# A fused attention and expert kernel: attention's features transposed on VectorE from raw rows, row deviation applied after the products, K's elu as a sum on GpSimd

## The chip, the cores and the metric

The kernel runs on one core of a Trainium2 chip, in one launch. Its time is the device time of that core, in microseconds (us), from the first to the last instruction and what lies around them; the median of several runs counts. The engines are PE (TensorE, matrix products and transposes), DVE (VectorE), ACT (ScalarE), POOL (GpSimd) and SP (SyncE, which here only issues DMAs). Each works through its own instructions in program order.

## The reference

For 16 batches of 1024 tokens with 256 features, a row is normalized, and a linear attention with 16 heads of 16 and a layer of 8 experts are both added to the raw row:

```
xn  = (x - mean(x)) / sqrt(var(x) + 1e-5)
Q, K = elu(xn Wq' + bq) + 1, elu(xn Wk' + bk) + 1 ;  V = xn Wv' + bv
attn = per head  Q (K' V) / (Q . sum(K) + 1e-6),  then Wo' + bo
probs = softmax(xn gate_w)                  # over the 8 experts
g, m  = top 256 tokens of each expert in each batch, by probs
ffn[m] += g * (gelu(xn[m] w1[e]) w2[e])     # scatter-add over experts
out = x + attn + ffn
```

All inputs and the output are 32-bit floats.

## The kernel before

**Attention** runs first, one batch per step, `step(b)` for b from -1 to 16. It is a software pipeline: in step b the K products and the gate are made for batch b+1 (`next_`), Q, the denominators and K'V for batch b (`here`), the output for b-1 (`prev`), and the row statistics, the normalized rows and their transposes for b+2 (`ahead`). x of b+3 is loaded. Products with V's and the output's weights are folded into 256x256 matrices (`folded_k`, `folded_v`, `folded_o`).

The order on every engine is written out by hand: within `tc.manual_schedule` each engine keeps the order of the calls. The names that matter: `moments` (L272) and `deviations` (L276 to L281: aggregation and the negated mean on DVE, the deviation by a power on POOL), `normalize` (L295, ACT), `transpose_x` (L306 on PE, L311 copies out of PSUM on ACT) makes `xnT`, in which the features lie on the partitions; `key` (L319 PE, L323 DVE: bias added while reading PSUM) fills `kk`, whose last 8 columns are the gate's logits; `exp_of` (L328, L329) makes exp(min(t, 0)) in two ACT operations; `elu` (L333, DVE) takes the larger of that and t+1, the 1 being part of the bias; `gate_exp` and `gate` (L341 to L357) do the softmax on DVE with its exponent on ACT, and SP stores the row with its probabilities; `key_sum` (L366 to L368, POOL) adds K over the tokens; `query` (L388 PE, L393 DVE), `query_keys` (L401, POOL), `divide` (L409 to L413 on DVE, L415 on POOL), `folded_k` (L424), `transpose_q` (L470, L473), `project` (L494, L500). The DVE part of a step is in this order: K's reads with the moments between them, deviations, gate's maximum, elu of K's first half, gate, Q's first read, elu of K's second half, Q's second read, third read, elu of Q's first half, fourth read, elu of Q's second half, the two divisions, the outputs.

From step 3 to step 14, rounds of the top-k search of the first four batches (L188 to L193, on DVE) are put in between, eight instructions a step (`top`). PSUM has eight banks, which are handed out in rotation by `bank`.

**Experts.** 64 units follow, each one expert with 2 batches. A unit gathers 512 rows by indirect DMA on POOL (`gather`, L238), SP regroups them in blocks of 32 partitions (`quadrants`, L712), DVE transposes 32x32 blocks (`transposed`, L721), and both layers are done by a seven-product scheme (`layer1` L798, `layer2` L877), whose sums lie on DVE and POOL (`fourth_sum`, L863, feeds the last product of `layer2`). The result, weighed on ACT (L894), is added into `acc` in DRAM by indirect DMA on POOL (`scatter`, L900). `plan` places the pieces of the output (x + attention + bias + acc, in parts of 256 rows: `load_a`, `cast` L1017, `bias` L1021, `add` L1026, `store` L1030) into slots of the units ("s1" to "s4", "first", "middle", "lay"). The parts of the last unit's batches wait for its scatters and a reload of `acc` (`load_last_a`, L1013).

Of the kernel before, what the change touches and what calls it, by code (L numbers as in the profile page):

```python
# [23 lines left out]
def tile_linear_attn_expert_choice_moe(  # L24
# [72 lines left out]
    wo_sb = const.tile([P, NC, E], F32, name="wo_sb")  # L97
    bqc = const.tile([P, NC], F32, name="bqc")
# [4 lines left out]

    def load_first_weights():
        nc.scalar.dma_start(wkg_sb[:, :, 0:E], wkT.rearrange("(c p) o -> p c o", p=P))
        nc.scalar.dma_start(wkg_sb[:, :, E:KG], gate_w.rearrange("(c p) e -> p c e", p=P))
        nc.gpsimd.memset(bk_sb[:, E:KG], 0.0)
        nc.scalar.dma_start(bk_sb[:, 0:E], bk.partition_broadcast(P))

    def load_other_weights():  # L110
        nc.sync.dma_start(wq_sb, wqT.rearrange("(c p) o -> p c o", p=P))
# [4 lines left out]
        nc.sync.dma_start(bo_sb, bo.partition_broadcast(P))  # L116


    def add_one():
        nc.gpsimd.tensor_scalar(bk_sb[:, 0:E], bk_sb[:, 0:E], 1.0, None, ALU.add)  # L120

    def spread_bq(diag):

        for c in range(NC):
            nc.vector.tensor_scalar(diag[:, c, :], ident, bqc[:, c : c + 1], None, ALU.mult)
# [6 lines left out]
    def load_w1(g, e):  # L132
        w1_sb = wpool.tile([P, NC, HID], F32, tag="w1", name=f"w1_{g}_{e}")

        wq4 = w1[e].rearrange("(q c i) f -> q i c f", q=4, c=NC)
        for q in range(4):
            nc.sync.dma_start(w1_sb[32 * q : 32 * q + 32, :, :], wq4[q])
# [107 lines left out]
    def attention(xpool, apool, tpool, zpool, first_units):  # L245
# [3 lines left out]
        class Batch:  # L249
            def __init__(self, b):  # L250
                self.b = b

        def load_x(t):
# [4 lines left out]
            for g in range(2):  # L258
                nc.sync.dma_start(
                    t.x[g],  # L260
                    x[t.b].rearrange("(j p) d -> p j d", p=P)[:, 4 * g : 4 * g + 4, :],
                )

        def new_stats(t):
# [3 lines left out]
            t.rstd = tpool.tile([P, NJ], F32, tag="rstd", name=f"rstd{t.b}")  # L268
# [31 lines left out]
        def transpose_x(t, g):  # L300
            if g == 0:
                t.xnT = xpool.tile([P, NC, S], F32, tag="xnT", name=f"xnT{t.b}")
            for c in range(NC):
                pt = bank(f"xt{t.b}_{g}_{c}")
                for j in range(4):
                    nc.tensor.transpose(  # L306
# [4 lines left out]
                nc.scalar.copy(t.xnT[:, c, g * 512 : (g + 1) * 512], pt)  # L311


        def key(t, j):
# [3 lines left out]
            for d in range(NC):  # L318
                nc.tensor.matmul(  # L319
                    pk[:, 0:KG], t.xnT[:, d, j * P : (j + 1) * P], wkg_sb[:, d, :],  # L320
                    start=(d == 0), stop=(d == NC - 1),
                )
            nc.vector.tensor_tensor(t.kk[:, j, :], pk[:, 0:KG], bk_sb, ALU.add)  # L323


        def exp_of(t, name, g, of):
            e = tpool.tile([P, 4, E], F32, tag="e", name=f"{name}e{t.b}_{g}", bufs=3)
            nc.scalar.activation(e, of, AF.Relu, bias=1.0, scale=-1.0)  # L328
# [3 lines left out]
        def elu(of, e):  # L332
            nc.vector.tensor_tensor(of, of, e, ALU.max)  # L333

# [892 lines left out]
```

## Time and profile before

| | |
|---|---|
| median of 3 runs | 2173.39 us (2169.7 to 2173.79) |
| profiled execution | 2174.56 us, its span 2172.8 us |
| TensorE clock granted | 0.994 of full speed |
| attention | 0 to about 556 us; steps 3 to 13 take 33.53 us each |
| experts | from 558 us |
| last product of layer 2 ends | about 2146.3 us |

A line of a timeline gives the start and duration in us, the engine, the line of the kernel, the operation, what is written and read, and the shapes; in brackets stands how long the engine had been idle and what released it. In the windows, the first two numbers are the stretch and its length, then the busy time of PE, PE's weight loads, DVE, ACT and POOL with the number of instructions, the granted clock, the share of DMA time and GB/s.

### The profile page before, as it was taken

What the parts mean: (1) busy time and instruction counts of PE and PEld (TensorE: products, weight loads), DVE (VectorE), ACT (ScalarE), POOL (GpSimd) and SP (SyncE); (2) the same over time, 40 slices, a digit from 0 to 9 for tenths busy, and PEclk for the clock granted to TensorE, in tenths of its full rate; (3) what the DMA queues carried; (4) which work ended last, traced back from release to release, by engine and by line L of the source; (5) the groups of instructions that cost most, each with busy time, mean ns of one, the idle gap of its engine ahead of it and who ended that gap; (6) DMA issues with size and microseconds to landing.
All of it is one profiled execution on the core that took longest, in us unless ns stands there. A gap on an engine that the chain in (4) does not pass through costs nothing.

```text
span 2172.8 us, 37223 instructions
## 1 busy us (share of the span) xinstructions
PE 2125.9 (98%) x13556; PEld 1958.3 (90%) x13556; DVE 1754.6 (81%) x3197; ACT 860.9 (40%) x1599; POOL 1354.7 (62%) x1015
## 2 busy tenths in 40 slices
PE   7999999999999999999999999999999999999995
PEld 6888888888899998999999999899999999999994
DVE  6888888887799888679999998767777788777786
ACT  5645546453333333333333333333333333333334
POOL 4545445454677777677666766676676667667743
PEclk9999999999999999999999999999999999999998
DMA  6444535455555555454565556445546665565567
GB/s 200 138 146 147 188 125 176 156 161 173 122 108 103 104 113 124 102 122 94 135 137 118 119 133 135 77 92 106 115 103 165 166 156 115 132 140 106 117 168 213
DMA packets 333767, 290.61 MB, mean 134 GB/s; under 512 B 163856, under 2 KB 285968, under 8 KB 333584
## 3 DMA queue, kind: packets, MB, share of 16 engines
q1 hardware_dynamic: 283168, 217.55, 35.3%
q0 software_dynamic: 49728, 70.29, 18.5%
q8 instruction: 107, 1.75, 0.4%
q14 instruction: 76, 0.62, 0.1%
q10 hardware_dynamic: 688, 0.40, 0.1%
HBM read 153.36 MB, written 101.19 MB: 117 GB/s over the span
## 4 chain that ended last, share of the span: by engine, by line
PE 97%; DVE 1%; DMA 1%; issue 0%; ACT 0%; POOL 0%; SPq 0%; POOLq 0%; DVEq 0%; ACTq 0%
PE pb L798 15%; PE qz L877 11%; PE qx L877 11%; PE pc L798 10%; PE pa L798 10%; PE pk L319 5%; PE qv L877 5%; PE qw L877 5%; PE qy L877 5%; PE pq L388 5%; PE pg L424 5%; PE po L494 5%; PE xt L306 1%; PE qt L470 1%; PE pv L439 1%; PE pm L458 1%
## 5 line engine op out<-in xcount | busy, mean ns | idle before, releaser
L900 POOL DMA_INDIRECT acc<-y,idxT x256 | 414.9, 1621 | 349.8 <-ACT y L894 172.5
L238 POOL DMA_INDIRECT rows<-xg,idxT x256 | 261.4, 1021 | 77.6 <-issue 69.4
L894 ACT ACTIVATE y<-y,rows 128x256 f32<-128x256 f32 (+1 forms) x256 | 102.5, 448 | 516.1 <-DVE y L932 514.7
L773 ACT ACTIVATE hT<-hT 128x512 f32<-128x512 f32 x384 | 237.9, 630 | 154.5 <-DVE hT L830 92.0
L798 PE MATMUL pb<-ts,ws 128*128 128x256 f32 x1024 | 264.7, 381 | 1.9 <-DVE ts L748 1.2
L798 PE MATMUL pa<-xT,w 128*128 128x256 f32 x1024 | 263.7, 380 | 1.1 <-issue 1.1
L877 PE MATMUL qx<-w,hT 128*128 128x128 f32 x2048 | 249.5, 275 | 0.0
L877 PEld LDWEIGHTS qx<-w,hT 128*128 128x128 f32 x2048 | 243.9, 192 | 3.3
L863 POOL TENSOR_TENSOR sums<-hT,sums 128x512 f32<-128x512 f32 x128 | 172.3, 1363 | 96.6 <-PE qz L877 96.2
L798 PEld LDWEIGHTS pb<-ts,ws 128*128 128x128 f32 x1024 | 195.3, 191 | 29.3 <-POOL wt L767 1.6
L798 PEld LDWEIGHTS pa<-xT,w 128*128 128x128 f32 x1024 | 190.2, 191 | 24.6 <-issue 1.3
L828 DVE TENSOR_TENSOR u<-pb,p 128x512 f32<-128x512 f32 x128 | 88.4, 691 | 114.9 <-PE pb L798 99.6
L773 ACT ACTIVATE hT<-pa 128x512 f32<-128x512 f32 x128 | 76.4, 597 | 177.2 <-PE pa L798 175.8
L819 DVE TENSOR_TENSOR u<-pb,p 128x512 f32<-128x512 f32 x128 | 88.5, 691 | 65.6 <-ACT y L894 41.4
L812 ACT COPY p<-pa 128x512 f32<-128x512 f32 x128 | 74.9, 585 | 166.3 <-PE pa L798 157.5
L798 PE MATMUL pc<-xT,ws 128*128 128x256 f32 x512 | 134.7, 385 | 0.9 <-DVE hT L830 0.9
L798 PE MATMUL pc<-ts,ws 128*128 128x256 f32 x512 | 132.7, 382 | 0.0
L798 PE MATMUL pb<-ts,w 128*128 128x256 f32 x512 | 131.4, 379 | 0.0
L877 PE MATMUL qz<-w,sums 128*128 128x128 f32 x1024 | 124.9, 275 | 0.0
L877 PE MATMUL qw<-wt,hT 128*128 128x128 f32 x1024 | 124.8, 275 | 0.0
L877 PE MATMUL qz<-wt,sums 128*128 128x128 f32 x1024 | 124.8, 275 | 0.0
L877 PE MATMUL qv<-wt,hT 128*128 128x128 f32 x1024 | 124.8, 275 | 0.0
(145 smaller groups left out, 4747.6 us busy)
## 6 DMA issues: line engine op xcount, KB each, us to landing
rq<-rows SPq DMA_DIRECT2D x1024, 32.0 KB
w<-in_w_dram SPq DMA_DIRECT2D x96, 256.0 KB
w<-in_w_dram SPq DMA_DIRECT2D x48, 512.0 KB
xg<-xn SPq DMA_DIRECT2D x16, 1056.0 KB
x<-in_x_dram SPq DMA_DIRECT2D x32, 512.0 KB
acc<-zero SPq DMA_DIRECT2D x16, 1024.0 KB
xr<-in_x_dram SPq DMA_DIRECT2D x30, 512.0 KB
xa<-xr SPq DMA_DIRECT2D x28, 512.0 KB
```

The source lines that it names most:

```text
L238: nc.gpsimd.indirect_dma_start(out=rows[:, q, :], out_offset=None, in_=xg[b], in_offset=bass.IndirectOffsetOnAxis(ap=ix, axis=0),)
L319: nc.tensor.matmul(pk[:, 0:KG], t.xnT[:, d, j * P : (j + 1) * P], wkg_sb[:, d, :], start=(d == 0), stop=(d == NC - 1),)
L388: nc.tensor.matmul(pq[:, k * E : (k + 1) * E], t.xnT[:, d, j * P : (j + 1) * P], wq_sb[:, d, :], start=(d == 0), stop=(d == NC - 1),)
L424: nc.tensor.matmul(t.pg[:, c * E : (c + 1) * E], t.xn[:, j, c * P : (c + 1) * P], t.kk[:, j, 0:E], start=(j == 0), stop=(j == NJ - 1),)
L494: nc.tensor.matmul(po[:, k * E : (k + 1) * E], qT[:, c, j * P : (j + 1) * P], t.mo[:, c, :], start=(c == 0), stop=(c == NC - 1),)
L773: nc.scalar.activation(out, in_, AF.Gelu_apprx_tanh)
L798: nc.tensor.matmul(bk[:, j * HT : (j + 1) * HT], w[:, f * P : (f + 1) * P], x, start=start and j == 0, stop=True, skip_group_check=True,)
L819: nc.vector.tensor_tensor(u2, both(pb), p1, ALU.add)
L863: nc.gpsimd.tensor_tensor(u.half_sum(0, r), u.block(1, 0, r), u.half_sum(1, r), ALU.subtract)
L877: nc.tensor.matmul(bk[:, k * EH : (k + 1) * EH], a[:, c, k * P : (k + 1) * P], b[:, c, :], start=start and k == 0 and c == 0, stop=True, s ...
L894: nc.scalar.activation(y[:, k, cols], in_, AF.Copy, scale=rows[:, q, E + u.e : E + u.e + 1])
L900: nc.gpsimd.indirect_dma_start(out=acc[b], out_offset=bass.IndirectOffsetOnAxis(ap=ix, axis=0), in_=y[:, k, :], in_offset=None, compute_op ...
```

## The change

In attention, for batches from 2 on, `xnT` is no longer made from normalized rows on PE. x is loaded a second time by `load_blocks`, in runs of 64 features (256 bytes) to blocks of 32 partitions, and `transpose_blocks` lets DVE transpose 32x32 blocks of it; so `xnT` holds raw x. The mean is taken out of the weights instead: `center` subtracts the mean over the input features from each column of second copies of Wk, gate and Wq. The deviation `rstd` of a row is multiplied in by `of_tokens` when K and Q are read from PSUM. Batches 0 and 1 keep the old way with the uncentered copies. K's elu becomes relu(t) + exp(min(t, 0)): `split_key` does three ACT operations, and `elu_key` the sum, on POOL (on DVE in step -1).

At the start, x of batch 0 is loaded in quarters, its statistics are taken in pairs of row groups, `warm_up` puts matmuls of ones on PE ahead of the first transposes, and the second half's transposes follow the first half's K. At the turn to the experts, the second gather moves behind the divisions, the third in front of the second layer's weight sums, and the first expert's w1 is loaded a step later. At the end, the last unit doesn't scatter: `new_hot` and `fill_hot` make one-hot matrices of its token indices in earlier units (`iota` on POOL, a comparison on DVE), `spread` multiplies them with the unit's result on PE, and DVE adds `acc`, which is loaded before that. The last unit's `fourth_sum` runs on DVE, and some biases, additions and stores move into it.

The diff, cut to its core:

```diff
+    def load_in_blocks(queue, tile_, w):
+        w4 = w.rearrange("(q c i) f -> q i c f", q=4, c=NC)
+        for q in range(4):
+            queue.dma_start(tile_[32 * q : 32 * q + 32, :, :], w4[q])
+
+
+    def center(w, n):
+        pb = bank("pw")
+        for c in range(NC):
+            nc.tensor.matmul(
+                pb[:, 0:n], ones, w[:, c, :], start=(c == 0), stop=(c == NC - 1)
+            )
+        for c in range(NC):
+            nc.vector.scalar_tensor_tensor(
+                w[:, c, :], pb[:, 0:n], -1.0 / E, w[:, c, :], ALU.mult, ALU.add
+            )
...
+        load_in_blocks(nc.sync, wkg_sb[:, :, 0:E], wkT)
+        load_in_blocks(nc.sync, wkg_sb[:, :, E:KG], gate_w)
+        load_in_blocks(nc.sync, wq_sb, wqT)
...
+            n = 2 if t.b == 0 else 4
+            for j in range(0, NJ, n):
...
+                    t.x[j // 4][:, i : i + n, :],
+                    x[t.b].rearrange("(j p) d -> p j d", p=P)[:, j : j + n, :],
+                )
+
+        def load_blocks(t):
+
+
+            t.blocks = wpool.tile([P, NC, HID], F32, tag="w1", name=f"xb{t.b}").rearrange(
+                "p c (s d) -> p (c s) d", d=E // 4
+            )
+            x4 = x[t.b].rearrange("(s i) (q d) -> q i s d", i=32, q=4)
+            for q in range(4):
+                nc.sync.dma_start(t.blocks[32 * q : 32 * q + 32, :, :], x4[q])
+
+        def transpose_blocks(t, g):
+            if g == 0:
+                t.xnT = xpool.tile([P, NC, S], F32, tag="xnT", name=f"xnT{t.b}")
+            n = S // 64
+            for c in range(NC):
+                nc.vector.transpose(
+                    t.xnT[:, c, g * 512 : (g + 1) * 512].rearrange("p (s i) -> p s i", i=32),
+                    t.blocks[:, g * n : (g + 1) * n, 32 * c : 32 * c + 32],
                 )
...
+        def warm_up(n):
+            for _ in range(n):
+                nc.tensor.matmul(warm[:, 0:P], ones, ones, start=True, stop=True)
...
+                    if t.b == 0 and g == 0 and c == 0 and j > 1:
+                        warm_up(3)
...
+                t.pt[c] = pt
+                if copies:
+                    copy_x(t, g, c)
+
+        def copy_x(t, g, c=None):
+            for c in range(NC) if c is None else (c,):
+                nc.scalar.copy(t.xnT[:, c, g * 512 : (g + 1) * 512], t.pt[c])
...
+        def of_tokens(t, j, out_, in_, bias):
+            if t.b < 2:
+                nc.vector.tensor_tensor(out_, in_, bias, ALU.add)
+            else:
+                nc.vector.scalar_tensor_tensor(
+                    out_, in_, t.rstd[:, j : j + 1], bias, ALU.mult, ALU.add
+                )
...
-                    pk[:, 0:KG], t.xnT[:, d, j * P : (j + 1) * P], wkg_sb[:, d, :],
+                    pk[:, 0:KG], t.xnT[:, d, j * P : (j + 1) * P], (wkg_0 if t.b < 2 else wkg_sb)[:, d, :],
...
-            nc.vector.tensor_tensor(t.kk[:, j, :], pk[:, 0:KG], bk_sb, ALU.add)
-
-
-        def exp_of(t, name, g, of):
+            of_tokens(t, j, t.kk[:, j, :], pk[:, 0:KG], bk_sb)
...
-            nc.scalar.activation(e, of, AF.Relu, bias=1.0, scale=-1.0)
+            nc.scalar.activation(e, of, AF.Relu, bias=one, scale=-1.0)
...
+        def split_key(t, g):
+            e = exp_of(t, "k", g, khalf(t, g), 0.0)
+            nc.scalar.activation(khalf(t, g), khalf(t, g), AF.Relu)
+            return e
+
+        def elu_key(t, g, e, engine):
+            engine.tensor_tensor(khalf(t, g), khalf(t, g), e, ALU.add)
...
-            nc.vector.tensor_tensor(
-                t.q[g][:, 2 * i : 2 * i + 2, :],
-                pq.rearrange("p (t d) -> p t d", t=2),
-                bq_sb.unsqueeze(1).to_broadcast([P, 2, E]), ALU.add,
-            )
+            for k in range(2):
+                of_tokens(
+                    t, 4 * g + 2 * i + k, t.q[g][:, 2 * i + k, :],
+                    pq[:, k * E : (k + 1) * E], bq_sb,
+                )
...
             if b + 3 < B:
                 load_x(ts[b + 3])
+                load_blocks(ts[b + 3])
...
-                first["w1"] = load_w1(*first_units[0][0:2])
                 first["w2"] = load_w2(wpool, *first_units[0][0:2])
...
             if b == B - 2:
+                first["w1"] = load_w1(*first_units[0][0:2])
...
+                if early and j == 3:
+                    transpose_x(ts[0], 1)
+                    normalize(ahead, halves[0], shared=True)
+                if early and j == 5:
+                    spread_bq(diag)
+                    center(wkg_sb, KG)
+                    center(wq_sb, E)
                 if next_ and j == 3:
-                    ke0 = exp_of(next_, "k", 0, khalf(next_, 0))
+                    ke0 = split_key(next_, 0)
+                    if early:
+                        normalize(ahead, halves[1], shared=True)
+                if early and j == 6:
+                    transpose_x(ahead, 0)
+            if early:
...
             if next_:
-                ke1 = exp_of(next_, "k", 1, khalf(next_, 1))
+                ke1 = split_key(next_, 1)
...
-            if here:
+            if here and b:
                 key_sum_all(here)
...
-                elu(khalf(next_, 0), ke0)
+                elu_key(next_, 0, ke0, nc.vector if early else nc.gpsimd)
                 gate(next_)
...
             if next_:
-                elu(khalf(next_, 1), ke1)
+                elu_key(next_, 1, ke1, nc.vector if early else nc.gpsimd)
                 key_sum(next_)
...
-            if ahead:
-                transpose_x(ahead, 0)
+            if early:
+                copy_x(ahead, 1)
+            elif ahead:
+                transpose_blocks(ahead, 0)
             if here:
                 elu(here.q[1], qe1)
                 qk1 = query_keys(here, 1)
-            if b == B - 1:
-                first["rows"].append(gather(*first_units[1]))
...
-            if ahead:
-                transpose_x(ahead, 1)
+            if ahead and not early:
+                transpose_blocks(ahead, 1)
             if here:
                 folded_k(here, 1)
                 divide(here, 1, qk1)
                 clear(here)
+            if b == B - 1:
+                first["rows"].append(gather(*first_units[1]))
             top(1)
...
+        warm_up(12)
         t = ts[0]
-        for g in range(2):
-            for j in range(4 * g, 4 * g + 4):
-                moments(t, j)
-            deviations(t, halves[g])
-        add_one()
-        for g in range(2):
-            normalize(t, halves[g], shared=True)
-            transpose_x(t, g)
-        t = ts[1]
-        for j in range(NJ):
-            moments(t, j)
-        deviations(t, every)
-        normalize(t, every)
+        pairs = []
+        for lo in (0, 2):
+            pairs.append(measure(t, lo, lo + 2))
+            deviations(t, pairs[-1])
+        normalize(t, pairs[0], shared=True)
+        half = measure(t, 4, NJ)
+        normalize(t, pairs[1], shared=True)
+        deviations(t, half)
+        transpose_x(t, 0)
+        deviations(ts[1], measure(ts[1], 0, 4))
+        normalize(t, half, shared=True)
...
-        def fourth_sum(u, r):
-            nc.gpsimd.tensor_tensor(
+        def fourth_sum(u, r, engine):
+            engine.tensor_tensor(
                 u.half_sum(0, r), u.block(1, 0, r), u.half_sum(1, r), ALU.subtract
...
+            if not final:
+                scatter(y1, 1, 0)
                 more_sums()
                 scatter(y1, 1, 1)
...
+                if not final:
+                    scatter(y0, 0, 0)
+                    between()
+                    scatter(y0, 0, 1)
+
+            u.y = (y0, y1)
...
+                    nc.gpsimd.iota(
+                        t, pattern=[[1, n], [NJ, P]], base=i * n, channel_multiplier=0,
+                        allow_small_or_imprecise_dtypes=True,
+                    )
+                self.hot[q] = [t[:, j, :] for t in parts for j in range(n)]
+                self.hot_parts[q] = parts
+
+            def fill_hot(self, q):
+                h, e, b0 = units[-1]
+                _, ix = index(e, b0, q)
+                nc.vector.tensor_copy(self.slots[:, q : q + 1], ix)
+                for t in self.hot_parts[q]:
+                    nc.vector.tensor_scalar(
+                        t, t, self.slots[:, q : q + 1], None, ALU.is_equal
+                    )
...
+            def spread(self, p, y, t):
+                _, js = self.todo[p]
+                pr = bank(f"pr{p}")
+                for i, j in enumerate(range(js.start, js.stop)):
+                    for k in range(NS):
+                        nc.tensor.matmul(
+                            pr[:, i * E : (i + 1) * E], self.hot[t * NS + k][j], y[:, k, :],
+                            start=(k == 0), stop=(k == NS - 1),
+                        )
+                self.s[p] = hpool.tile([P, 2, E], BF16, tag="fb", name=f"fb{p}", bufs=5)
+                nc.vector.tensor_tensor(
+                    self.s[p], pr.rearrange("p (j d) -> p j d", j=2), self.a[p], ALU.add
+                )
...
             put(NU - 3, "first", done.load_last_x)
+            put(NU - 1, "first", done.load_last_a)
+            put(NU - 6, "s3", done.new_hots_first)
+            put(NU - 2, "s3", done.new_hot_last)
+            for q, at_ in enumerate(
+                [(NU - 4, "s2"), (NU - 4, "s4"), (NU - 3, "s2"), (NU - 1, "lay")]
+            ):
+                put(*at_, done.fill_hot, q)
...
+            for p in second[0:3]:
+                put(NU - 1, "s4", done.add, p)
+                put(NU - 1, "s4", done.store, [p])
...
-            for s in sums:
+            for s in sums[0:4]:
+                s()
+            rows[2] = gather(*units[2])
+            for s in sums[4:]:
...
-                if not n:
-                    between()
...
-                done.add(p)
-                done.store([p])
+                if k >= 3:
+                    done.add(p)
+                    done.store([p])
             for step in at.pop((NU, "end")):
                 step()
-            done.load_last_a()
-            for p in last:
-                done.cast(p)
+            for k, p in enumerate(last):
+                done.spread(p, u.y[1 - k // QT], 1 - k // QT)
                 done.add(p)
                 done.store([p])
```

## The prediction

> **What bounds the kernel now.** The page's busy row and the chain that ended last come first: both put TensorE (PE) on the path nearly everywhere.
>
> ```profile
> PE 2125.9 (98%) x13556; PEld 1958.3 (90%) x13556; DVE 1754.6 (81%) x3197; ACT 860.9 (40%) x1599; POOL 1354.7 (62%) x1015
> PE 97%; DVE 1%; DMA 1%; issue 0%; ACT 0%; POOL 0%; SPq 0%; POOLq 0%; DVEq 0%; ACTq 0%
> ```
>
> The change is mostly in attention (0 to about 556 us), so next the timeline of PE through one attention step, and the table of windows for a step:
>
> ```profile
> 254.18 7.28 PE L319 MATMUL pk<-wkg_sb,xnT 128*128 128x264 f32 x32
> 271.25 1.04 PE L306 MATMUL xt<-ident,xn 128*128 128x128 f32 x8
> 272.12 3.62 PE L424 MATMUL pg<-kk,xn 128*128 128x256 f32 x16
> 275.57 1.04 PE L306 MATMUL xt<-ident,xn 128*128 128x128 f32 x8
> 287.70 7.28 PE L319 MATMUL pk<-wkg_sb,xnT 128*128 128x264 f32 x32
> ...
> 254.34:287.87 33.53, 33.53 (x175) 29.71 (x175) 28.18 (x66) 17.76 (x28) 15.93 (x10) 1.00 0.47 158
> ```
>
> A step lasts 33.53 us and PE (second number) fills all of it, but DVE (fourth, VectorE) is busy 28.18 of it. How DVE's 5 us of gaps arise decides this case, so I read DVE and POOL (GpSimd) in the same step:
>
> ```profile
> 255.99 0.42 DVE L323 TENSOR_TENSOR kk<-pk,bk_sb 128x264 f32<-128x264 f32 x1
> 263.31 1.22 DVE L333 TENSOR_TENSOR kk<-kk,ke 128x1024 f32<-128x1024 f32 x1
> 265.23 0.22 DVE L350 TENSOR_REDUCE sm<-ex 128x8 f32<-128x64 f32 x1 [0.69 <-ACT ex L346]
> 270.71 2.14 DVE L333 TENSOR_TENSOR q<-q,qe 128x1024 f32<-128x1024 f32 x1 [1.18 <-ACT qe L329]
> 275.67 1.23 DVE L333 TENSOR_TENSOR q<-q,qe 128x1024 f32<-128x1024 f32 x1 [2.21 <-ACT qe L329]
> 289.50 0.42 DVE L323 TENSOR_TENSOR kk<-pk,bk_sb 128x264 f32<-128x264 f32 x1
> ...
> 268.05 2.37 POOL L366 TENSOR_TENSOR s<-kk 128x1024 f32<-128x1024 f32 x1 [2.84 <-DVE kk L333]
> 270.50 1.28 POOL L367 TENSOR_TENSOR s<-s 128x512 f32<-128x512 f32 x1
> 271.85 1.59 POOL L368 TENSOR_TENSOR s<-s 128x256 f32<-128x256 f32 x1
> ```
>
> DVE waits for ACT (ScalarE) three times, in program order, with everything behind it queued. And the first elu of Q takes 2.14 us instead of 1.23: it begins while POOL adds, and ends 1.07 us after POOL's L367 does; POOL's next add (L368) is stretched in turn.
>
> **The change, attention.** *PE.* Each step for batch 2 to 15 loses two groups of 8 transposes, 272.12 - 271.25 = 0.87 us each: 1.74 a step, 24.4 us over 14 steps. A step would be 31.8.
> *DVE.* Out: two elus of K, 1.14 start to start each, 2.3. In: four 128x512 transposes; L721 has that form, 0.68 long, 0.6 apart, 2.4. The four Q bias reads of 128x512 (0.60 apart) become eight of 128x256 (0.34): +0.5. Sixteen reads become scalar_tensor_tensor; L446 at 128x128 (0.33, some 0.04 over what L323's rate gives): +0.6. Net +1.2.
> *ACT.* Four copies of xt out (2.1); two Relus of 128x1024 in (1.06 each). Equal in sum, but the copies stand behind everything and the Relus in front: K's chain is now three operations, 3.1 us, twice, ahead of the exponent that the gate waits for.
> *POOL.* Two 128x1024 adds in, 2.37 each by L366, in front of key_sum and the first q*ks.
> *SP and DMA.* Four issues a step (about 0.4 each) and 4096 packets of 256 B. In the step's window 4901 packets took 48.2% of 16 engines; between 1000 and 1050 us, among the experts, 6692 packets of the same queue, most of them 256 B, took 33.7% of 16 engines, 40 ns each. That adds about 10 us of the 16 engines, 47% to nearly 80%. A block is used a whole step after its issue, so I cost it at nothing; without that cover a late block would stop DVE, and PE behind it.
>
> Is DVE's own round, if PE were never late, now longer than PE's 31.8? Count from the first K read (0), each engine in its order. For the step as it is: fourth K read ends 2.4, ACT's two operations 4.5, qT copies 5.5, second pair 7.5, gate's exponent 7.8; DVE does its K elu meanwhile, then gate, Q reads, K elu, Q read, 11.1; ACT's qe 13.2; Q elu behind POOL 15.2; Q read, qe 18.1; elu 19.4; from there to the next K read 12.7 (276.81 to 289.50): 32.1. That is under 33.5, so PE sets the time, as the trace says, with only 1.4 to spare.
> After: fourth read 2.6, three operations 5.7, qT 6.6, three more 9.7, exponent 10.0. DVE, with no K elu to do, stands still for 3 us at the gate. Gate and Q reads to 12.4, ACT's normalization to 12.7, qe 14.8. If both Q elus keep today's lengths (2.14 and 1.23): 16.9, Q read 17.7, qe 19.8, elu 21.0; then 12.7 and two transposes (1.2): 34.9. The first pair of transposes fits into the wait for qe.
> Here a rule weighs in. The Trainium skill ("SBUF — State Buffer", section "Who interferes with whom") says that a VectorE instruction with two SBUF inputs and a GpSimd instruction that reads SBUF exclude each other, the second waiting for the whole of the first. L333's 2.14 fits that. By it, POOL, now adding without a break from about 8.6 to 21.5, stops the first Q elu until 16.0 (ends 17.1) and the second until 21.5 (ends 22.6): 36.5. The gate's small operations meet the K adds too; that delay is partly absorbed, since it moves the elu into a better place. By the row +1.3 a step, by the rule +3.0; I take 36.0, +2.5, nearer the rule as the row shows it.
> That holds for steps 3 to 13, where top-k puts 5.5 us on DVE: 11 x 2.5 = +27. Steps 0 to 2 have no top-k: some 31 to 32, so nearly PE's time, -4 of the possible -5.2. Step 14 has no transposes: +1 for the longer ACT and POOL chain.
>
> **The ends.** *Start:* pairs of rows, warm-up matmuls and K of the first half before the second half's transposes. Cold groups of 8 transposes took 2.04 against 0.87, and K starts at 15.0. K could start 3 us sooner, but ACT (eight copies, Relus) and the centering (4 matmuls and 4 DVE operations, behind weights that 12 further issues on SP, some 5 us, bring last) follow; PE and DVE would both stand behind a late weight. Between -5 and +2: -2.5.
> *Turn to the experts:* the second gather goes behind POOL's divisions; now DVE's kv (L450) takes 3.8 us behind those and PE waits 1.1: -1. The third gather moves in front of the wt sums, 5 us on POOL, wanted only at 575.6: 0; w1's load, one step later, still lands 50 us early: 0.
> *End:*
>
> ```profile
> 2146.38 0.42 DVE L944 TENSOR_TENSOR y<-qz,u_y 128x256 f32<-128x256 f32 x1 [2.36 <-PE qz L877]
> 2153.98 2.10 POOL L900 DMA_INDIRECT acc<-y,idxT  x1 [2.71 <-issue]
> 2158.68 0.62 ACT L1017 CAST fb<-fa_rq 128x512 bf16<-128x512 f32 x1 [9.08 <-DMA fa_rq<-acc]
> 2165.96 2.02 DVE L1026 TENSOR_TENSOR fx_ws<-fx_ws,fb 128x512 f32<-128x512 f32 x3 [2.06 <-ACT fb L1017]
> ```
>
> The scatters and the reload of acc go. Instead PE does 32 matmuls (0.22 each, 7 us) and DVE 5 remaining adds, a bias and 8 times two operations: (6 + 16) x 0.62 = 13.6 from 2146.8, so 2160.4 instead of 2168.0: -7.6. The one-hots: POOL fills 4096 elements a partition (between the memset row, 0.52 for 512, and the add, 1.28: 4 to 10 us, three quarters in one place ahead of L863), DVE four comparisons of 1024 (0.7 to 1.2). With 5 us of slack a unit on either, 0 to 5: +1.5. What moves into the last unit (two fourth sums, 1.4 us on DVE, three adds, two biases, one comparison; eight loads of acc on SP, 0.4 each, ahead of others) goes into DVE's gaps there, 5 us between 2138 and 2146.4; if they are too small, up to 3 us of the -7.6 are lost.
>
> **Sum.** -4 + 27 + 1 - 2.5 - 1 - 7.6 + 1.5 = +14.4 on the profiled execution's 2174.6: 2189.0; the median of the runs shown is 1.2 below it, so 2188.
>
> **The rivals.** (1) *PE stays the bound.* All 14 steps give 1.74: -24.4 - 2.5 - 1 - 7.6 + 1.5 = -34: 2139. For it: PE has no wait in the step now, and DVE's sum, some 29.4, is below 31.8. It decides once DVE's round is under 31.8, 4.2 below my count; the three waits for ACT, 5 us together, would have to vanish. Against it: they are serial and in order. 18%.
> (2) *The round is longer, the locks hardly bite.* With both Q elus at 1.23 it is 33.9: +4 in steps 3 to 13, total -9: 2165. 13%.
> (3) *The small loads bite as well:* at 80% of the DMA engines x or residuals come late, 1 to 2 us a step more: 2205 to 2220. The lead of a whole step speaks against it. 7%.
> My forecast has 62%, with its own range of 2172 to 2208.
>
> **How the numbers follow.** A change under 0.2% (4 us) can't be told from none here. Faster: rival 1, nearly all of 2, little of mine: 0.31. Same: 0.05. Slower: 0.64. To leave out no more than 2 in 10 the range must reach into rival 1: 2142 to 2212.
>
> **What would show it.** In a step of 3 to 13: period 35 to 37, PE waiting for DVE at pk or po, DVE idle about 3 us before sm (releaser ex on ACT), Q elus of 2 us or more with POOL's K adds of 2.4 in front; in steps 1 and 2 some 32. From the last product of layer 2 to the end some 19 us instead of 26. A period of 31.8 with PE full proves me wrong.

## The result, and the profile after

| | before | after |
|---|---|---|
| median | 2172.27 us (2169.7 to 2173.79) | 2205.85 us (2203.74 to 2208.03) |
| profiled execution | 2174.56 us | 2203.74 us |

The changed kernel is slower: the ratio is 1.0156, with a 95% interval of 1.0138 to 1.0173. The profiled execution of the changed kernel is the fastest of its runs and that of the kernel before slower than the other runs of it shown here, so the profiles lie 29.2 us apart where the medians lie 33.6 apart. Busy times and the chain that ended last, on the page of the changed kernel, and the row of the table of windows for step 6 (stretch, its length, then busy time of PE, PE's weight loads, DVE, ACT, POOL; granted clock, share of DMA time, GB/s):

```profile
PE 2139.2 (97%) x13440; PEld 1952.4 (89%) x13440; DVE 1798.4 (82%) x3317; ACT 854.3 (39%) x1563; POOL 1419.0 (64%) x1050
PE 71%; DVE 16%; ACT 6%; issue 2%; SPq 2%; DMA 2%; POOL 0%; DVEq 0%; ACTq 0%; POOLq 0%
...
234.89:271.51 36.62, 32.84 (x160) 27.59 (x159) 30.70 (x72) 17.49 (x26) 20.75 (x12) 1.00 0.70 173
```

PE was on 97% of the chain and is on 71% now. In the step it is the first number after the comma: 32.84 busy in 36.62, with nearly 4 us of waiting, where before it had none. The clock is full in this step (1.00), so this isn't a slower PE. No busy share tells the cause: DVE is busy 30.70 of 36.62, waits for ACT in most of the rest, and its round still sets the time. The same step in the timelines of DVE, POOL, ACT and PE of the changed kernel (start, duration; in brackets the idle time before and what ended it):

```profile
234.89 0.48 DVE L377 SCALAR_TENSOR_TENSOR kk<-pk,rstd,bk_sb 128x264 f32<-128x264 f32 x1
244.87 0.22 DVE L427 TENSOR_REDUCE sm<-ex 128x8 f32<-128x64 f32 x1 [2.95 <-ACT ex L423]
245.36 0.77 DVE L430 TENSOR_TENSOR xn<-ex,rs 128x64 f32<-128x64 f32 x1
246.16 2.25 DVE L434 COPY probs<-xn 128x64 f32<-128x64 f32 x1
252.19 1.23 DVE L401 TENSOR_TENSOR q<-q,qe 128x1024 f32<-128x1024 f32 x1 [1.43 <-ACT qe L397]
256.48 1.23 DVE L401 TENSOR_TENSOR q<-q,qe 128x1024 f32<-128x1024 f32 x1 [1.06 <-ACT qe L397]
271.51 0.48 DVE L377 SCALAR_TENSOR_TENSOR kk<-pk,rstd,bk_sb 128x264 f32<-128x264 f32 x1
...
243.68 4.68 POOL L410 TENSOR_TENSOR kk<-kk,ke 128x1024 f32<-128x1024 f32 x2
248.44 2.37 POOL L443 TENSOR_TENSOR s<-kk 128x1024 f32<-128x1024 f32 x1
250.89 1.28 POOL L444 TENSOR_TENSOR s<-s 128x512 f32<-128x512 f32 x1
252.24 1.77 POOL L445 TENSOR_TENSOR s<-s 128x256 f32<-128x256 f32 x1
253.97 2.38 POOL L479 TENSOR_TENSOR qk<-q,ks 128x1024 f32<-128x1024 f32 x1
...
243.65 1.04 ACT L406 ACTIVATE kk<-kk 128x1024 f32<-128x1024 f32 x1
244.60 0.24 ACT L423 ACTIVATE ex<-ex 128x64 f32<-128x64 f32 x1
255.39 1.06 ACT L397 ACTIVATE qe<-qe 128x1024 f32<-128x1024 f32 x1
...
267.50 2.05 PE L387 MATMUL pk<-wkg_sb,xnT 128*128 128x264 f32 x8 [2.27 <-DVE xr L578]
```

Read it from the top. The gate's sum waits 2.95 us for its exponent, which stands on ACT behind the two times three operations of K's elu (the last of them is ACT's L406 at 243.65). The copy of the probabilities, 64 elements a partition, takes 2.25 us and ends at 248.41, just after POOL's second K add (243.68 + 4.68 = 248.36); in e1 below, with no add on POOL, it takes 0.20. POOL then works without a break until 256.35, and ACT makes the second exponent of Q until 256.45 (255.39 + 1.06): both chains end just ahead of DVE's second elu of Q at 256.48. PE's K products at 267.50 waited 2.27 us for an output read on DVE: that is how DVE's round reaches PE.

Where the 29.2 us between the two profiled executions lie is read from the first K read of each step on DVE (the first and last line of DVE above are two of them):

| | before | after | difference |
|---|---|---|---|
| first K read of step 3 | 121.15 | 124.98 | +3.8 |
| from there to that of step 14 | 369.5 | 403.0 | +33.4 |
| from there to the end of the span | 1682.1 | 1674.1 | -8.0 |

### The profile page after: what moved, and what is told of

Its sections match the earlier page's. It is cut to its first block, busy times and chain, and to the rows that moved or that the text cites. A ratio compares the mean times of both kernels' runs of the same rounds, so it can differ in the third digit from the quotient of the medians.

```text
span 2202.0 us, 37264 instructions
## 1 busy us (share of the span) xinstructions
PE 2139.2 (97%) x13440; PEld 1952.4 (89%) x13440; DVE 1798.4 (82%) x3317; ACT 854.3 (39%) x1563; POOL 1419.0 (64%) x1050
## 4 chain that ended last, share of the span: by engine, by line
PE 71%; DVE 16%; ACT 6%; issue 2%; SPq 2%; DMA 2%; POOL 0%; DVEq 0%; ACTq 0%; POOLq 0%
PE pb L899 15%; PE qz L978 10%; PE pc L899 10%; PE qx L978 10%; PE pa L899 10%; PE qw L978 5%; PE qv L978 5%; PE qy L978 5%; DVE den L487 2%; DVE xr L578 2%; SPq L297 1%; ACT qe L396 1%; ACT qe L397 1%; DVE q L377 1%; DVE probs L434 1%
## 5 line engine op out<-in xcount | busy, mean ns | idle before, releaser
L1001 POOL DMA_INDIRECT acc<-y,idxT x252 | 407.3, 1616 | 349.6 <-ACT y L995 192.8
L259 POOL DMA_INDIRECT rows<-xg,idxT x256 | 262.1, 1024 | 77.8 <-issue 70.1
L387 PE MATMUL pk<-wkg_sb,xnT 128*128 128x264 f32 x448 | 117.3, 417 | 27.7 <-DVE xr L578 25.0
L387 PEld LDWEIGHTS pk<-wkg_sb,xnT 128*128 128x128 f32 x448 | 89.8, 205 | 52.5 <-DVE xr L578 31.4
```

The source lines that it names most:

```text
L259: nc.gpsimd.indirect_dma_start(out=rows[:, q, :], out_offset=None, in_=xg[b], in_offset=bass.IndirectOffsetOnAxis(ap=ix, axis=0),)
L387: nc.tensor.matmul(pk[:, 0:KG], t.xnT[:, d, j * P : (j + 1) * P], (wkg_0 if t.b < 2 else wkg_sb)[:, d, :], start=(d == 0), stop=(d == NC - 1),
L1001: nc.gpsimd.indirect_dma_start(out=acc[b], out_offset=bass.IndirectOffsetOnAxis(ap=ix, axis=0), in_=y[:, k, :], in_offset=None, compute_op ...
```

## The experiments

Three theories on the 37 us in attention: **A**, K's elu (a third operation on ACT ahead of the gate's exponent, two sums on POOL in front of everything that DVE does with two operands from SBUF); **B**, DVE's own new work (four transposes, split Q reads); **C**, the loads of 256 bytes. In the table a round is the mean distance between the first K reads of steps 4 to 14, and the rest runs from the last of these to the end of the span; ratios are against the kernel before on the same chip.

| kernel | step 3 begins | round | rest | median us | ratio (95%) |
|---|---|---|---|---|---|
| before | 121.15 | 33.53 | 1682.1 | 2172.27 | |
| after | 124.98 | 36.64 | 1674.1 | 2205.85 | 1.0156 (1.0138 to 1.0173) |
| e1_kelu_old | 115.78 | 33.94 | 1671.3 | 2163.59 | 0.9959 (0.9945 to 0.9973) |
| e2_kadd_dve | 121.36 | 35.78 | 1673.1 | 2190.13 | 1.0082 (1.0065 to 1.0099) |
| e3_ends_only | 116.49 | 33.53 | 1671.0 | 2160.61 | 0.9946 (0.9929 to 0.9962) |
| e4_kelu_alone | 126.33 | 34.65 | 1684.1 | 2195.29 | 1.0105 (1.0088 to 1.0121) |
| e5_gate_late | 127.47 | 37.04 | 1673.1 | 2209.56 | 1.0178 (1.0161 to 1.0195) |
| e6_reordered | 121.58 | 34.83 | 1675.2 | 2178.62 | 1.0028 (1.0016 to 1.0039) |
| e7_old_elu_reads_first | 115.69 | 33.73 | 1672.1 | 2159.66 | 0.9946 (0.9929 to 0.9963) |
| e8_old_elu_dodged | 114.94 | 31.78 | 1669.7 | 2139.54 | 0.9848 (0.9832 to 0.9865) |
| e9_new_elu_dodged | 120.23 | 31.78 | 1673.6 | 2148.74 | 0.9890 (0.9873 to 0.9906) |

### e1_kelu_old: all of the change but K's elu

```diff
         def split_key(t, g):
-            e = exp_of(t, "k", g, khalf(t, g), 0.0)
-            nc.scalar.activation(khalf(t, g), khalf(t, g), AF.Relu)
-            return e
+            return exp_of(t, "k", g, khalf(t, g))
         def elu_key(t, g, e, engine):
-            engine.tensor_tensor(khalf(t, g), khalf(t, g), e, ALU.add)
+            nc.vector.tensor_tensor(khalf(t, g), khalf(t, g), e, ALU.max)
...
+        nc.gpsimd.tensor_scalar(bk_sb[:, 0:E], bk_sb[:, 0:E], 1.0, None, ALU.add)
```

> The changed kernel with K's elu as it was (two ScalarE operations, larger-of on VectorE, 1 in the bias); VectorE's transposes, the deviation behind the products and both ends stay. Theory A (K's elu is the damage: its third ScalarE operation delays the gate, and its sums on GpSimd block the gate's product and copy): VectorE's round falls from 36.6 to about 34.0, and steps 0, 1 and 14 lose their excess too: 2165 to 2172 us. Theory B (the damage is what VectorE got: transposes, finer reads with the deviation): VectorE now has 2.3 us of elu more, so the round stays at 36.6 or grows: 2205 or more. Theory C (the small loads slow everything): no change, 2205.

2163.59, faster than before, and a round of 33.94. Its timeline, DVE and POOL:

```profile
226.10 1.22 DVE L408 TENSOR_TENSOR kk<-kk,ke 128x1024 f32<-128x1024 f32 x1
227.98 0.20 DVE L432 COPY probs<-xn 128x64 f32<-128x64 f32 x1
233.09 1.94 DVE L401 TENSOR_TENSOR q<-q,qe 128x1024 f32<-128x1024 f32 x1 [1.43 <-ACT qe L397]
238.03 1.23 DVE L401 TENSOR_TENSOR q<-q,qe 128x1024 f32<-128x1024 f32 x1 [1.00 <-ACT qe L397]
...
230.24 2.37 POOL L441 TENSOR_TENSOR s<-kk 128x1024 f32<-128x1024 f32 x1 [2.22 <-DVE kk L408]
```

The copy is 0.20 again, and DVE does K's two elus (1.22 each) in time that the changed kernel spends waiting for the gate. DVE carries more work here than in the changed kernel (31.00 us busy in step 6, against 30.70 that contain the stretched copy) and its round is 2.7 us shorter. The transposes on DVE and the small loads are all still there: theories B and C fall as explanations of the loss. That 42 us of the changed kernel are K's elu follows from this one run.

### e2_kadd_dve: K's sum back on DVE, the third operation stays on ACT

```diff
-            engine.tensor_tensor(khalf(t, g), khalf(t, g), e, ALU.add)
+            nc.vector.tensor_tensor(khalf(t, g), khalf(t, g), e, ALU.add)
```

> The changed kernel with K's sum on VectorE in all steps instead of GpSimd; ScalarE still does three operations. If the blocking by GpSimd is nearly all of it: like e1, 2165 to 2172. If ScalarE's longer chain in front of the gate weighs as much: the gate is no longer blocked but still waits until 10 us for the exponent, and VectorE has the sums again: round about 35.8, 2190 to 2197. Theory B: 2215 or more.

2190.13, a round of 35.78. DVE's copy is back at 0.20 and the wait for the gate's exponent at 1.75, with an elu of K in front of it. So ACT's third operation alone costs 1.8 us a round against e1, and the sum on POOL another 0.9; in this order of the operations the split is worse than the old form with its sum on either engine.

### e3_ends_only: attention's steps as before, start, turn and end as changed

```diff
             elif ahead:
-                transpose_blocks(ahead, 0)
+                transpose_x(ahead, 0)
...
-                load_blocks(ts[b + 3])
...
-            if t.b < 2:
+            if True:
                 nc.vector.tensor_tensor(out_, in_, bias, ALU.add)
```

(the second pair of transposes, Q's reads and K's elu likewise, and the centered weights left out)

> The changed kernel with attention's steps as before (transposes on TensorE, one weight layout, K's elu as before): only the start, the turn to the experts and the end are changed. The two profiles give the start 3.3 us less, the experts with the end 8.7 less: 2159 to 2163. If these gains exist only because attention runs late: 2172.

2160.61: the steps take 33.53 as before, step 3 begins 4.7 us sooner, and the rest is 11.1 shorter. The parts of the change outside the steps are a gain of 12 us by the medians (15.8 between the two profiles). So inside them the change loses 2205.85 - 2160.61 = 45.

### e4_kelu_alone: only K's elu, in the kernel before

```diff
-                    ke0 = exp_of(next_, "k", 0, khalf(next_, 0))
+                    ke0 = split_key(next_, 0)
...
-                elu(khalf(next_, 0), ke0)
+                elu_key(next_, 0, ke0, nc.vector if early else nc.gpsimd)
...
-        add_one()
```

(`split_key` and `elu_key` as in the change; the second half likewise)

> The kernel before with K's elu alone changed (three ScalarE operations, sum on GpSimd). Theory A: VectorE's round, counted as for the prediction, is 34.6 against TensorE's 33.5, step 14 has its long gate too: 2184 to 2192. Theory B and C: TensorE hides it, 2172.

2195.29: slower by 22 us, with nothing else changed. The timeline of DVE in its step 6:

```profile
241.56 0.22 DVE L358 TENSOR_REDUCE sm<-ex 128x8 f32<-128x64 f32 x1 [3.19 <-ACT ex L354]
242.61 2.26 DVE L365 COPY probs<-xn 128x64 f32<-128x64 f32 x1
```

The two marks of the changed kernel, the wait at the gate and the copy of over 2 us, appear without its transposes. A holds on both sides: taken out of the change, and put into the kernel before.

### e5_gate_late: which of the marks costs the time

A had two readings. Either DVE's visible losses at the gate (5 us) are the cost (theory D of the expectation), or they are only where a longer chain shows (theory E: POOL's K adds, key sums and first q*ks, during which DVE's elus of Q can't run). The gate alone is moved:

```diff
-                gate(next_)
+                if early:
+                    gate(next_)
...
                 transpose_blocks(ahead, 1)
+            if next_ and not early:
+                gate(next_)
```

> The changed kernel with one thing moved: the gate of the next batch (sm, rs, xn, probs, its DMA) stands behind VectorE's second pair of transposes, where GpSimd is idle, in place of ahead of the Q reads. In the changed kernel the gate costs VectorE 2.95 us of waiting for the exponent, and 2.25 us for a copy of 0.20. Theory D (the gate's delay is the loss): without it VectorE is 5 us ahead, so a step of 3 to 13 falls from 36.6 to 31.8 (TensorE's own round) and the time from 2206 to about 2150. Theory E (GpSimd's chain is the loss: two K adds of 2.34, three key sums of 2.4, 1.3 and 1.7 and the first q*ks of 2.4 run without a gap, and the second elu of Q starts when they end): the gate only stood in a gap that is there anyway; the second elu still starts at the end of the q*ks, some 21.5 us after the step's first K read, and the gate's 0.9 us now lie behind it: 36.6 to 37.5 a step, 2204 to 2216.

2209.56, a round of 37.04: D falls. The timeline of DVE and POOL:

```profile
253.32 2.29 DVE L401 TENSOR_TENSOR q<-q,qe 128x1024 f32<-128x1024 f32 x1 [4.05 <-ACT qe L397]
258.67 2.29 DVE L401 TENSOR_TENSOR q<-q,qe 128x1024 f32<-128x1024 f32 x1 [1.06 <-ACT qe L397]
268.23 0.20 DVE L434 COPY probs<-xn 128x64 f32<-128x64 f32 x1
...
252.16 2.36 POOL L443 TENSOR_TENSOR s<-kk 128x1024 f32<-128x1024 f32 x1
257.52 2.36 POOL L479 TENSOR_TENSOR qk<-q,ks 128x1024 f32<-128x1024 f32 x1
```

The gate costs nothing extra now (the copy is 0.20), and the time saved goes into waiting: 4.05 us before the first elu of Q, then both elus last 2.29, each ending 1.1 us after the POOL operation that it met (252.16 + 2.36 = 254.52 and 255.61; 259.88 and 260.96). From the step's first K read, at 238.59, the second elu ends after 22.4 us; in the changed kernel after 22.8 (257.71 - 234.89). The gate's loss of 5 us had been cover for something almost as long: without it the second elu ends 0.4 sooner, and the gate's 0.9 us come later in the round. A stall seen on an engine isn't its price.

### e6_reordered: POOL's and ACT's chains shortened as well

The gate stands as in e5, the key sums behind both q*ks, the last Q reads ahead of the first elu of Q, and the normalizations of ACT behind the copies of qT (first half) and behind `folded_k` (second half):

```diff
-                key_sum(next_)
...
-                elu(here.q[0], qe0)
-                qk0 = query_keys(here, 0)
                 query(here, 1, 1)
+                elu(here.q[0], qe0)
+                qk0 = query_keys(here, 0)
+                qe1 = exp_of(here, "q", 1, here.q[1])
...
                 qk1 = query_keys(here, 1)
+                key_sum(next_)
```

> The changed kernel with the same operations in another order: the gate as in e5_gate_late, the three key sums on GpSimd behind both products q*ks, the last Q reads on VectorE ahead of the first elu of Q, the two normalizations on ScalarE behind the Q elus. By theory E the chain of GpSimd ahead of the second elu of Q falls by 5.4 us, and ScalarE's exponents of Q come 2 to 4 us sooner: VectorE's round is counted at 30.8, under TensorE's 31.8, so TensorE sets the step: 31.8 to 32.3, first K read of step 3 some 5 us sooner too, the time 2140 to 2152. By theory D this gains no more over e5_gate_late than 1 us a step. A rest (round of 33 or more) would mean that the operations that exclude each other (GpSimd's adds and VectorE's elus) still meet.

2178.62 and a round of 34.83: 27 us gained over the changed kernel, about half or less of what was counted (54 to 66). DVE and POOL:

```profile
242.44 2.38 DVE L401 TENSOR_TENSOR q<-q,qe 128x1024 f32<-128x1024 f32 x1
247.36 2.26 DVE L490 TENSOR_SCALAR den<-den 128x64 f32<-128x64 f32 x1
...
241.37 2.36 POOL L479 TENSOR_TENSOR qk<-q,ks 128x1024 f32<-128x1024 f32 x1 [1.16 <-DVE q L401]
247.22 2.35 POOL L443 TENSOR_TENSOR s<-kk 128x1024 f32<-128x1024 f32 x1
```

The second elu of Q now ends 18.1 us after the step's first K read, 4.7 sooner; ACT's and POOL's chains were shortened together, so how much of it is either's alone stays open. But it met the first q*ks, and the key sum that was moved away from the elus met the 64-element addition in the divisor: 2.26 in place of 0.20. The sum 36.64 - 4.7 + 0.9 (the gate in its new place) + 2.1 = 34.9 is the round measured. My count had let the second elu pass beside the q*ks, and had forgotten the operation with one operand.

### e7_old_elu_reads_first

e1 with the last Q reads ahead of the first elu of Q:

```diff
-                elu(here.q[0], qe0)
-                qk0 = query_keys(here, 0)
                 query(here, 1, 1)
+                elu(here.q[0], qe0)
+                qk0 = query_keys(here, 0)
+                qe1 = exp_of(here, "q", 1, here.q[1])
             if ahead and not early:
                 normalize(ahead, halves[1])
```

> The changed kernel with K's elu as before (e1_kelu_old, round 33.9), and one thing moved: the last two Q reads stand on VectorE ahead of the first elu of Q, and ScalarE's second normalization behind the second pair of Q's exponents. VectorE waits 1.43 and 1.00 us for ScalarE there; the reads (0.86) fill the first wait and start the second exponents sooner. Count: 33.9 - 1.7 = 32.2 a step, near TensorE's 31.8: 2163.6 - 11 x 1.7 = 2145 (2140 to 2150). If the waits only move (VectorE late elsewhere), 33.5 or more and 2160.

2159.66, a round of 33.73, 0.2 less than e1 in place of 1.7: a miss. DVE no longer waited for the second exponent, and met POOL instead (timelines of both):

```profile
235.77 2.86 DVE L401 TENSOR_TENSOR q<-q,qe 128x1024 f32<-128x1024 f32 x1
...
235.18 2.36 POOL L477 TENSOR_TENSOR qk<-q,ks 128x1024 f32<-128x1024 f32 x1
```

The elu could begin at 235.77, POOL had begun 0.59 earlier, and the elu ended at 238.63, 1.09 after POOL's end: its own length, almost exactly, once POOL was done.

### e8_old_elu_dodged and e9_new_elu_dodged: next to nothing meets

The operations that ran at full length beside POOL (transposes, the searches of top-k) are put where POOL adds, the others where it is idle, and POOL's first q*ks can't start before both elus of Q are done, since the second half's goes first. e8 is e1 with:

```diff
                 query(here, 1, 1)
+                qe1 = exp_of(here, "q", 1, here.q[1])
...
                 transpose_blocks(ahead, 0)
+            top(2)
             if here:
+                elu(here.q[0], qe0)
                 elu(here.q[1], qe1)
                 qk1 = query_keys(here, 1)
-            top(2)
-            if here:
+                qk0 = query_keys(here, 0)
                 folded_k(here, 0)
-                divide(here, 0, qk0)
             top(3)
             if ahead and not early:
                 transpose_blocks(ahead, 1)
             if here:
-                folded_k(here, 1)
                 divide(here, 1, qk1)
+                folded_k(here, 1)
+                divide(here, 0, qk0)
```

e9 has the same on the changed kernel; its gate stands ahead of `elu(here.q[0], qe0)`, its `key_sum` behind the divisions, its normalizations as in e6.

> The changed kernel with K's elu as before and the operations that exclude each other pulled apart: on VectorE, after the last Q reads, the first pair of transposes and one search of top-k (they ran at full length beside GpSimd's adds in every trace so far), then both elus of Q one after the other; GpSimd's q*ks begin with the second half, so that the first starts only when both elus are done; the divisors last, the second half's first. In e7_old_elu_reads_first the gain of the reads was lost to one meeting: the second elu of Q took 2.86 us in place of 1.23, ending 1.1 us after GpSimd's first q*ks. Theory E (what excludes each other sets the round): both elus 1.23, no wait at the divisors; round counted at 31.1 to 31.8, so TensorE's own 31.8 sets the step from the first on, and VectorE no longer ends 7 us behind TensorE: 2160 - 17 - 5 = 2138 (2132 to 2146). Rival F (TensorE does not reach 31.8 while 256-byte loads and transposes run): 33 or more a step, 2150 to 2160.

> The same order for the changed kernel with K's elu as it has it (third operation on ScalarE, sum on GpSimd). The gate stands between GpSimd's K adds and the Q elus, where GpSimd is idle, the key sums behind the divisions, the normalizations on ScalarE behind the Q elus. Theory E: nothing in the split of K's elu is lost for good, it is a matter of where its sums fall; count 31 to 32.5 a step against 34.8 in e6_reordered: 2138 to 2152, at most 8 us over e8_old_elu_dodged. Rival G (the added work itself, 3.1 us on ScalarE and 4.7 us on GpSimd a step, costs its length wherever it stands): 34 to 35 a step, 2170 to 2180.

2139.54 and 2148.74, both with a round of 31.78. The row of the table of windows for step 7 of e8, and its timeline of DVE, POOL and PE:

```profile
244.67:276.43 31.76, 31.76 (x160) 27.98 (x159) 31.09 (x74) 15.68 (x24) 15.10 (x10) 1.00 0.79 200
...
259.42 0.66 DVE L214 MATCH_REPLACE8 cur<-top,cur 64x512 f32<-64x512 f32 x1
260.73 2.33 DVE L401 TENSOR_TENSOR q<-q,qe 128x1024 f32<-128x1024 f32 x2
269.57 1.01 DVE L488 TENSOR_SCALAR den<-den 128x64 f32<-128x64 f32 x1
...
259.57 0.73 POOL L443 TENSOR_TENSOR s<-s 128x256 f32<-128x256 f32 x1
263.14 4.68 POOL L477 TENSOR_TENSOR qk<-q,ks 128x1024 f32<-128x1024 f32 x2 [2.84 <-DVE q L401]
...
240.97 7.28 PE L387 MATMUL pk<-wkg_sb,xnT 128*128 128x264 f32 x32
272.75 7.28 PE L387 MATMUL pk<-wkg_sb,xnT 128*128 128x264 f32 x32
```

PE is busy all 31.76 us, from K products to K products 31.78. Both elus together take 2.33, with POOL standing still for 2.84 on purpose; only a divisor's addition still meets POOL (1.01 in place of 0.20). Rivals F and G fall: PE runs at its own 31.8 with a DMA share of 0.79, and the split of K's elu costs nothing per step there, where PE sets the pace. What it still costs lies outside the steps from 4 on: step 3 begins 5.3 us later in e9 than in e8, and from the first K read of step 14 to the first expert product it takes 68.8 us in place of 64.6; from there to the end the two are alike (1604.8 and 1605.1). e8 beats both kernels, and is 21 us under e3: that is what the transposes on DVE are worth in this order.

## Why the prediction was right or wrong

The sign, the mechanism in the steps (a round of DVE longer than PE's, through ACT's third operation and POOL's sums) and most of the signs to look for were right; the size was half: +14.4 forecast against the profiled execution, +29.2 measured. Term by term:

| term | forecast | measured |
|---|---|---|
| start, the centering with it (to the first K read of step 0) | -2.5 | -0.2 |
| steps 0 to 2 | -4 | +4.0 |
| steps 3 to 13 | +27 | +33.4 |
| step 14 and turn to the experts | 0 | +0.6 |
| experts and end, one-hots included | -6.1 | -8.6 |

**Steps 0 to 2 is the term that failed most.** Here are the first K reads of steps 0, 1, 2 and 3 on DVE, of the kernel before and of the changed one:

```profile
29.53 0.42 DVE L323 TENSOR_TENSOR kk<-pk,bk_sb 128x264 f32<-128x264 f32 x1
57.61 0.42 DVE L323 TENSOR_TENSOR kk<-pk,bk_sb 128x264 f32<-128x264 f32 x1
87.18 0.43 DVE L323 TENSOR_TENSOR kk<-pk,bk_sb 128x264 f32<-128x264 f32 x1 [0.20 <-PE pk L319]
121.15 0.43 DVE L323 TENSOR_TENSOR kk<-pk,bk_sb 128x264 f32<-128x264 f32 x1
...
29.36 0.42 DVE L375 TENSOR_TENSOR kk<-pk,bk_sb 128x264 f32<-128x264 f32 x1
59.81 0.48 DVE L377 SCALAR_TENSOR_TENSOR kk<-pk,rstd,bk_sb 128x264 f32<-128x264 f32 x1
91.94 0.48 DVE L377 SCALAR_TENSOR_TENSOR kk<-pk,rstd,bk_sb 128x264 f32<-128x264 f32 x1
124.98 0.47 DVE L377 SCALAR_TENSOR_TENSOR kk<-pk,rstd,bk_sb 128x264 f32<-128x264 f32 x1
```

The round itself was foretold well: "some 31 to 32", and the changed kernel takes 30.5, 32.1 and 33.0, in the mean 31.9. What failed is what it was compared with. "-4 of the possible -5.2" gives each of these steps the 33.5 us of the later ones, as if PE filled them all; but before the change they took 28.1, 29.6 and 34.0, in the mean 30.5. In step 0 there is no output of an earlier batch yet, and PE comes from its K products to the next in 24.9 us (27.61 to 52.56). The same round is therefore a loss of 4.0 and no gain of 4. With K's elu in the old form (e1) these steps take 27.8, 29.5 and 30.3: all of the loss, and 4 us more, is K's elu. At the start, e3 reaches step 0 3.1 us sooner than the kernel before, as foretold; what e1 has beyond e3 ahead of step 0, mainly the second weights and their centering, takes back 1.7 of that and K's elu 1.2.

**Steps 3 to 13: a choice between two numbers.** The count by the rule of the Trainium skill ("SBUF — State Buffer", section "Who interferes with whom") was 36.5, the one by the row 34.9; I took 36.0, and 36.64 was measured. Eleven steps of 0.6 are the 6 us missing here: discounting the rule is the second step that failed. The rule's count hits the end of the second elu of Q (22.6 us after the first K read counted, 22.8 measured) by POOL's chain, which ends at 21.5 in both; the first elu ends 1.4 later than counted (18.5, not 17.1), since the copy of 2.25 was not in the count. The rule was right to the length of an instruction: in the rows of e5, e6 and e7 above, each of DVE's operations that met POOL ends about its own length after POOL's. The single 2.14 us row that I set against it was no contrary evidence: that elu met a short add of 1.28, not one of 2.4. The same section also names the copy and the operation with a scalar among those that can take part; I had looked up only instructions with two inputs. The copy (2.25 for 0.20) and e6's divisor (2.26 for 0.20) are these.

**"That delay is partly absorbed"**, of the gate's small operations: by e5 all but 0.4 us of it is absorbed.

**Signs.** Round 36.6 (35 to 37 foretold), PE waiting for DVE at pk, 2.95 us idle before sm: as foretold. Q elus of 2 us or more: not so, they last 1.23; behind the slow copy, and released by ACT both times, DVE comes just when POOL's operation has ended (252.17 before 252.19, 256.35 before 256.48). They are over 2 us in e5, where nothing holds DVE up.

**Costed at nothing, rightly:** the small loads (e8 runs at PE's pace with a DMA share of 0.79). SP's four issues take 6 to 9 us a step in these traces and not 1.6, and still no transpose waits for a block. The one-hots, +1.5, cost nothing that shows: from the first expert product to the end of layer 2's last, 1585.7 us against about 1587.9. But the kernel before has a clock of 0.83 in two stretches of 10 us there (560 to 570 and 860 to 870), about 3.4 us by estimate, and the changed kernel has none, so a cost of 1 us may be hidden. The end is near the forecast (20.0 from the last layer-2 product, 19 foretold):

```profile
2179.96 2.05 PE L978 MATMUL qz<-w,sums 128*128 128x128 f32 x16 [0.77 <-DVE y L1033]
```

It ends at 2182.0, the span at 2202.0.

**The rivals.** (1), PE stays the bound, gave 31.8 a step and 2139. e9, the same work in another order, has that step, 31.78, at 2148.74; that e8 comes to 2139.54 is luck, for it has K's elu in the old form. (2), locks that hardly bite, put 33.9 on a round with both Q elus at 1.23; they do last 1.23, at a round of 36.64, with the lock's time in the copy, and e5 to e7 show it in the elus themselves. (3), small loads, gave a time near the one measured, by a cause that e1 and e8 exclude: had I only compared times, it would have looked confirmed.

## What to carry to other kernels

Count the round of each in-order engine in its own order before believing that freed work on the busiest engine is a gain: here PE's round fell by 1.75 us, and DVE's came to lie 4.9 above it. Moving an elementwise operation to GpSimd is not free for VectorE even when GpSimd is idle half of the time: pull apart in time what excludes each other, and fill VectorE beside GpSimd's adds with what doesn't take part (transposes, top-k searches, reads of PSUM). And before a visible stall is removed, ask what else ends at the same moment; e5 took 5 us of stall away and gained nothing. And before a saving per step is multiplied, read how long each step took: the first three here were shorter than the rest.

## What was not expected of the hardware

A 128x64 copy between SBUF tiles takes 0.20 us, or 2.25 beside a GpSimd add of 2.34 that began before it; an addition of a constant on 64 elements 0.20 or 2.26. Transposes of 32x32 blocks (0.65 to 0.71 for 128x512), the searches of top-k (0.63 to 0.70) and the reads of PSUM with a per-row factor (0.46 to 0.49) kept their lengths in the traces of after, e1, e5, e6, e8 and e9, beside GpSimd's adds too. Between two GpSimd adds that stand directly behind one another, a waiting VectorE operation got its turn: in e5 the elu runs from 254.5 to 255.6 between two key sums, and the second of them, 1.28 long in the changed kernel, then lasts 2.14. Four DMA issues of 64-feature blocks keep SP for 6.3 us in step 6 and 7.5 in step 7, where 0.4 each had been estimated. An iota of 1024 elements a partition takes GpSimd 1.61 us, a comparison of as many 0.75 on VectorE.
